# Attention scores as products of 128 key columns, added in PSUM to turned bias sums

## The chip, the cores and the metric

One core of one Trainium2 chip runs the whole kernel. The metric is device time in microseconds (us), the median of several runs. A profile is one further execution, recorded by the hardware profiler; its span is the recorded part of that execution.

## The reference

Four layers follow each other on an image `x` of 2 x 512 x 32 x 32 in f32. The change lies in the first, a deformable attention with 8 heads of 64 channels: 1024 queries per image (the pixels) and 64 keys per image and head (sampled points). Its core, shortened:

```python
pos = grid_q[:, :, None, :] - grid_kv[:, None, :, :]
bias = jnp.sign(pos) * jnp.log1p(jnp.abs(pos))
bias = jax.nn.relu(bias @ cpb_w1 + cpb_b1)      # 2 -> 128
bias = jax.nn.relu(bias @ cpb_w2 + cpb_b2)      # 128 -> 128
bias = (bias @ cpb_w3 + cpb_b3)                 # 128 -> 1, for each query and key
sim = jnp.einsum('bhid,bhjd->bhij', qh, kh) + bias
attn = jax.nn.softmax(sim, axis=-1)
out = jnp.einsum('bhij,bhjd->bhid', attn, vh)
```

So every pair of query and key goes through a small network of three layers, and its result is added to the product of query and key before the softmax. What follows is a projection and an MLP, a linear attention (layer 1), a full attention over 1024 positions (layer 2) and a rank-one attention with a gate (layer 3).

## The kernel before, in words

**Engines.** TensorE (PE) multiplies and writes PSUM; VectorE (DVE) and ScalarE (ACT) read PSUM and work elementwise; GpSimd (POOL) and SyncE (SP) issue DMAs here. On TensorE a weight load (PEld) puts the stationary operand (`lhsT`) in place, and the moving operand (`rhs`) streams past it. Each f32 matmul of the source stands in the trace as two instructions, a transpose as one.

**The loop.** The first layer is one loop over 512 keys, taken as 8 groups `g` of 64. A group is a pair of heads (`k`, 128 channels) of an image `b`, so every group holds 64 keys for each of two heads. Keys are taken two at a time as `p`; each half-step is written `(n, when)`, where `n` is the key and `when` 0 or 1. For each `p`:

- `first` (line 344, DVE, L349) makes the first layer of the bias network, two instructions per key;
- `second` (line 609) is called four times. Each call runs 8 matmuls (16 instructions, L616) with 32 stationary columns, four of which work side by side on quarters of the array, into `ph`, which has two buffers. ACT evicts `ph` with a ReLU into `r` (L625);
- `combine` (DVE, L631), `join`, `shift` and `fold` (DMAs that add on arrival, L634, L641, L646) fold the 128 hidden units together into tiles `xs`;
- `third` (line 664, PE, L669), every eighth key, multiplies by the last layer and adds four `xs` into the sums `psim0` and `psim1`, which hold 32 keys each: partition = key and head and half of the queries, column = query (512).

**Order.** Everything in the loop is pinned in program order. `at(n, when, fn)` puts a piece of work at a half-step, `run` carries it out there, so each engine sees the order of the calls. No planner moves it. After the loop `started.clear()` ends the pinning, and the last group's softmax runs with the work that follows.

**Around the change**, for a group `g`:

- `prepare` (line 679) samples and projects the keys. `keys` (line 733, ACT, L742) copies them, scaled, into `kblk`, and `values` (DVE, L754) copies the values. For `g > 0` the plan puts `keys` at key 64(g-1)+51. `kblk` has two sets (`g % 2`), each of four blocks of 128 columns: key half `kb`, query half `half`. It is zeroed once (line 149), so that each head meets its own channels only. `keys` fills it with 8 small copies.
- `scores` (line 648, PE, L654), at key 64g+10, multiplies `kblk` (stationary) by 512 queries of `q` (moving), 4 matmuls, and thereby starts `psim0` and `psim1`.
- `third` adds the bias sums to them (`start=False`) at keys 64g+14 to 64g+70.
- `attend` (line 793) is planned from key n = 64(g+1)+7. `evict` (ACT, L804) copies each `psim` to SBUF as `simt`, which lies in the same memory as `e`. `flip` (PE, L814) turns it by 8 transposes of 128 x 128 in two PSUM tiles `psm`, one for each key half, so that a query becomes a partition. `top` (DVE, L825) takes the maximum of each half, L827 the larger of the two, `sub` (DVE, L831) subtracts it into `e`; `exp` (ACT, L841), `total` (DVE, L845), `inverse` (L848) and `norm` (ACT, L852) complete the softmax. `back` (PE, L858) turns the result, and `keep_` (ACT, L867) writes it over the group's queries in `q`.
- While that goes on, `chain(1, 2, 82, 78)` and `chain(2, 4, 206, 114)` (lines 925 and 926) compute the sampling points of later groups: 36 pieces `tap` on DVE (L226, L229) over the keys 4 to 81 and 92 to 205, then short steps on ACT, DVE and PE.

After the loop, L1036 multiplies the probabilities kept in `q` by the projected values.

Of the kernel before, what the change touches and what calls it, by code (L numbers as in the profile page):

```python
# [10 lines left out]
F32 = mybir.dt.float32  # L11
AF = mybir.ActivationFunctionType
ALU = mybir.AluOpType
AX = mybir.AxisListType
PSUM = bass.MemoryType.PSUM

P = 128
B, C, H, W = 2, 512, 32, 32
HW = H * W
# [3 lines left out]
DH = 64  # L23
J = 64
# [47 lines left out]
def conv_seq(  # L72
# [20 lines left out]
    nc = tc.nc  # L93
# [6 lines left out]
    x = keep.tile([P, KC, NT], F32, name="x")  # L100
# [22 lines left out]
    ident = c("ident")  # L123
# [10 lines left out]
    with ExitStack() as ctx_l0:  # L134
        l0 = ctx_l0.enter_context(tc.tile_pool(name="l0", bufs=1))
        q = l0.tile([P, KC, NT], F32, name="q")


        kblk = l0.tile([P, 2, 2, 2, P], F32, name="kblk")
        vblk = l0.tile([P, 2, 2, J], F32, name="vblk")  # L140

        co = l0.tile([P, 2, 2, KC * B * J], F32, name="co")
# [43 lines left out]
        def pin(ins):  # L186
            return tc.keep_in_program_order(ins) if started else ins
# [406 lines left out]
        with tc.tile_pool(name="hid", bufs=3) as hid, tc.tile_pool(name="sm", bufs=1) as sm, tc.tile_pool(name="hps", bufs=2, space=PSUM) as hps, tc.tile_pool(  # L594
# [6 lines left out]
            def at(n, when, fn, *args):  # L601

                todo.setdefault((n, when), []).append((fn, args))
# [41 lines left out]
                for i in range(2):  # L645
                    pin(nc.gpsimd.dma_start(rs[p][i::2], r[i::2, i, :], accum_op=ALU.add))  # L646

            def scores(g):
                k, b = divmod(g, B)
                for kb in range(2):  # L650
                    ps = psims[g, kb] = sps.tile([P, 512], F32, name=f"psim{kb}")
                    for half in range(2):
                        pin(
                            nc.tensor.matmul(  # L654
                                ps,
                                lhsT=kblk[:, g % 2, kb, half, :],
                                rhs=q[:, k, b * HW + half * 512 : b * HW + (half + 1) * 512],
                                start=(half == 0),
                                stop=False,
                                skip_group_check=True,  # L660
                            )
                        )

            def third(g, u):
                kb, i = divmod(u, 4)
                p = (g * J + 8 * u) // 2
                for m in range(4):
                    pin(
                        nc.tensor.matmul(  # L669
                            psims[g, kb][m * 32 : (m + 1) * 32, :],  # L670
                            lhsT=cw3[:, 3 - i : 35 - i],
                            rhs=rs.pop(p + m),
                            start=False,
                            stop=(i == 3),
                            skip_group_check=True,
                        )
                    )

            def prepare(g):

                k, b = divmod(g, B)
                st = {}
# [49 lines left out]

                def keys():

                    for half in range(2):
                        for h in range(2):
                            hs = slice(h * DH, (h + 1) * DH)
                            for kb in range(2):
                                to = kblk[hs, g % 2, kb, half, :].rearrange("p (m s c i) -> p s m c i", m=4, s=4, c=2)
                                of = st["pk"][hs, 0, kb * 32 : (kb + 1) * 32]  # L740
                                pin(
                                    nc.scalar.activation(  # L742
                                        to[:, 2 * half + h],
                                        of.rearrange("p (i m c) -> p m c i", i=4, m=4),
                                        AF.Identity,
                                        scale=DH**-0.5,
                                    )
                                )

                def values():  # L750
                    for h in range(2):
# [41 lines left out]
            def attend(g, n, step):  # L793

                k, b = divmod(g, B)
                st = {}

                def evict(kb):
                    if kb == 0:

                        st["e"] = sm.tile([P, 16, J], F32, name="e")
                        st["simt"] = st["e"].rearrange("p s j -> p (s j)").rearrange("p (k n) -> p k n", k=2)
                    pin(
                        nc.scalar.activation(  # L804
                            st["simt"][:, kb, :], psims[g, kb], AF.Identity, bias=v("L0_conv_cpb_b3")
                        )
                    )

                def flip(kb):

                    pt = st["pt", kb] = mps.tile([P, 4, 4, 4, 8], F32, name="psm", tag="m")
                    for t in range(4):
                        pin(
                            nc.tensor.transpose(  # L814
                                pt[:, t].rearrange("p s m i -> p m s i"), st["simt"][:, kb, t * P : (t + 1) * P], ident
                            )
                        )

                def top(kb):
                    if kb == 0:  # L820
                        st["mx"] = sm.tile([P, 2, 16], F32, name="mx")
                        st["den"] = sm.tile([P, 16], F32, name="den")
                    mx = st["mx"]
                    pt = st["pt", kb].rearrange("p t s m i -> p (t s) (m i)")
                    pin(nc.vector.tensor_reduce(mx[:, kb, :], pt, AX.X, ALU.max))  # L825
                    if kb == 1:
                        pin(nc.vector.tensor_tensor(mx[:, 0, :], mx[:, 0, :], mx[:, 1, :], ALU.max))  # L827

                def sub(kb):
                    pin(  # L830
                        nc.vector.tensor_tensor(  # L831
                            st["e"][:, :, kb * 32 : (kb + 1) * 32],
                            st["pt", kb].rearrange("p t s m i -> p (t s) (m i)"),
                            st["mx"][:, 0, :].unsqueeze(2).to_broadcast([P, 16, 32]),
                            ALU.subtract,
                        )
                    )

                def exp(t):
                    es = st["e"][:, t * 4 : t * 4 + 4, :]  # L840
                    pin(nc.scalar.activation(es, es, AF.Exp))  # L841

                def total(i):
                    is_ = slice(8 * i, 8 * i + 8)
                    pin(nc.vector.tensor_reduce(st["den"][:, is_], st["e"][:, is_], AX.X, ALU.add))  # L845

                def inverse():
                    pin(nc.vector.reciprocal(st["den"], st["den"]))  # L848

                def norm(i):  # L850
                    e = st["e"][:, i]
                    pin(nc.scalar.activation(e, e, AF.Identity, scale=st["den"][:, i : i + 1]))  # L852

                def back(s):
                    pb = st["pb", s] = mps.tile([P, 512], F32, name="pb", tag="m")
                    for t in range(4):
                        pin(
                            nc.tensor.transpose(  # L858
                                pb[:, t * P : (t + 1) * P],
                                st["e"][:, 4 * t + 2 * s : 4 * t + 2 * s + 2].rearrange("p h j -> p (h j)"),  # L860
                                ident,
                            )
                        )

                def keep_(s):

                    pin(nc.scalar.copy(q[:, k, b * HW + s * 512 : b * HW + (s + 1) * 512], st["pb", s]))  # L867

                plan = [
                    (0, 0, evict, 0), (0, 1, evict, 1), (1, 1, flip, 0), (1, 1, flip, 1),  # L870
                    (2, 1, top, 0), (3, 1, top, 1), (4, 1, sub, 0), (6, 1, sub, 1),
                    (10, 1, exp, 0), (11, 1, exp, 1), (12, 1, exp, 2), (13, 1, exp, 3),
                    (14, 1, total, 0), (16, 1, total, 1), (17, 1, inverse),
                ]
                plan += [(19 + i // 2, i % 2, norm, i) for i in range(16)]
                plan += [
                    (29, 0, back, 0), (29, 0, back, 1), (29, 1, keep_, 0), (30, 1, keep_, 1),
                ]
                for dn, when, fn, *args in plan:
                    if step:  # L880
                        at(n + dn, when, fn, *args)
                    else:
                        fn(*args)
# [13 lines left out]
                    )  # L897
            for g in range(NG):
                prepare(g)
                at(J * g + 10, 0, scores, g)  # L900
                for u in range(8):
                    at(J * g + 8 * u + 14, 0, third, g, u)
                if g < NG - 1:
                    attend(g, J * (g + 1) + 7, True)
# [830 lines left out]
```

## Time and profile before

| What | us |
|---|---|
| median of 3 runs | 2767.3 |
| lowest and highest run | 2765.76, 2767.45 |
| the profiled execution | 2764.49 |
| its span | 2762.7 |

The granted TensorE clock in the profiled execution was 0.996. Groups that the change touches, with the sum of busy time and the mean length of one instruction, from the trace:

| Line | Engine | Work | Count | Busy us | Mean ns |
|---|---|---|---|---|---|
| L616 | PE | `second` | 16384 | 1790.7 | 593 |
| L654 | PE | `scores` | 64 | 29.6 | 605 |
| L814 | PE | `flip` | 64 | 8.9 | 280 |
| L669 | PE | `third` | 512 | 72.1 | 592 |
| L742 | ACT | `keys` | 64 | 8.7 | 184 |
| L825 | DVE | `top` | 16 | 11.0 | 688 |
| L827 | DVE | larger of two maxima | 8 | 1.4 | 175 |

A matmul's length in the trace includes its way through the array; matmuls overlap, so busy time is less than count times mean, and the distance between starts tells what one costs in a stream. A busy PE is not PE at its peak. Rows of the trace in order of time read: start, length, engine, line, operation, output and inputs, shapes, count, and in brackets the idle time before it with what ended it.

### The profile page before, as it was taken

How to read it: one execution, taken by the hardware profiler on the slowest of the kernel's cores; microseconds unless marked ns; L12 is line 12 of the kernel's file. 1: busy time of each engine (PE TensorE's matmuls, PEld its weight loads, DVE VectorE, ACT ScalarE, POOL GpSimd, SP SyncE). 2: the span in 40 equal slices, each digit the busy share in tenths (PEclk: the TensorE clock that was granted, in tenths of full speed). 3: DMA queues.
4: the chain of work that ended last, by engine and by line, in shares of the span. 5: the costliest groups of instructions: out<-in, count | busy, mean ns of one | idle time of the engine just before them, and what ended most of it. 6: DMA issues, size and time to landing. Idle time of an engine off the chain costs nothing.

```text
span 2762.7 us, 49727 instructions
## 1 busy us (share of the span) xinstructions
PE 2707.0 (98%) x19782; PEld 987.5 (36%) x19782; DVE 2266.7 (82%) x2473; ACT 1544.3 (56%) x1950; POOL 663.6 (24%) x776
## 2 busy tenths in 40 slices
PE   8999999999999999999999999999999999999996
PEld 4233323233332323333333333333344444455543
DVE  6999999999999999999999999999654545523555
ACT  6676677667667776766776676676321111001244
POOL 0333333333333333333333333333100000000000
PEclk9999999999999999999999999999999999999998
DMA  3777777777777777777787778777400000100001
GB/s 121 160 163 155 161 154 160 158 160 158 154 164 149 162 163 158 161 161 156 167 185 172 152 165 193 154 170 159 102 30 23 16 23 23 70 7 0 0 1 61
DMA packets 145479, 335.14 MB, mean 121 GB/s; under 512 B 22592, under 2 KB 32064, under 8 KB 144480
## 3 DMA queue, kind: packets, MB, share of 16 engines
q0 software_dynamic: 77824, 201.38, 41.1%
q1 hardware_dynamic: 66992, 130.08, 13.2%
q8 instruction: 156, 2.56, 0.4%
q14 instruction: 75, 0.61, 0.1%
q10 hardware_dynamic: 432, 0.51, 0.1%
HBM read 58.99 MB, written 4.46 MB: 23 GB/s over the span
## 4 chain that ended last, share of the span: by engine, by line
PE 93%; ACT 3%; DVE 2%; issue 1%; DMA 1%; ACTq 0%; DVEq 0%; POOL 0%; SPq 0%; POOLq 0%
PE ph L616 61%; PE A L1101 4%; PE D L1101 4%; PE C L1101 4%; PE psim L669 2%; PE pr L1348 2%; PE B L1101 2%; PE po L1036 2%; PE pg L1244 1%; PE psim L654 1%; PE pz L1450 1%; PE pa L1339 1%; PE pu L1278 1%; ACT r L625 1%; PE pscore L1421 1%
## 5 line engine op out<-in xcount | busy, mean ns | idle before, releaser
L616 PE MATMUL ph<-h,w2a 128*32 128x512 f32 x16384 | 1790.7, 593 | 7.0 <-ACT r L625 6.9
L625 ACT ACTIVATE r<-ph,sb 128x1024 f32<-128x1024 f32 x1024 | 1141.4, 1115 | 562.3 <-PE ph L616 541.1
L349 DVE CUSTOM_DVE_ANT_1 h<-tab 128x1024 f32<-128x1024 f32 x1024 | 1205.9, 1220 | 8.6 <-PE ph L616 4.7
L616 PEld LDWEIGHTS ph<-h,w2a 128*32 128x32 f32 x16384 | 533.5, 109 | 1217.5 <-issue 833.1
L631 DVE SCALAR_TENSOR_TENSOR r<-r,rel,r 128x1024 f32<-128x1024 f32 x512 | 656.0, 1281 | 28.0 <-ACT r L625 27.3
L646 POOL DMA_DIRECT2D xs<-r x512 | 476.9, 1144 | 196.0 <-PE ph L616 95.7
L634 POOL DMA_DIRECT2D r<-r x256 | 222.2, 868 | 1107.2 <-DVE r L631 931.1
L172 ACT ACTIVATE tab<-tab,vec 128x256 f32<-128x256 f32 x252 | 137.1, 544 | 0.0
L1289 POOL MEMSET M<- 128x512 f32 x2 | 1.0, 520 | 439.6 <-DVE x L1165 439.6
L1141 ACT COPY u<-A 128x512 f32<-128x512 f32 x16 | 9.4, 585 | 146.9 <-PE A L1101 146.9
L1120 ACT ACTIVATE h<-h,vec 128x512 f32<-128x512 f32 x32 | 23.1, 721 | 113.6 <-DVE h L1123 113.6
L669 PE MATMUL psim<-xs,cw 128*32 128x512 f32 x512 | 72.1, 592 | 2.1 <-DMA xs<-r 2.1
L1123 DVE TENSOR_TENSOR h<-C,u 128x512 f32<-128x512 f32 x32 | 22.1, 691 | 48.8 <-PE C L1101 48.5
L1101 PE MATMUL A<-xn,w 128*128 128x512 f32 x128 | 60.2, 593 | 0.8 <-DVE x L1043 0.8
L1101 PE MATMUL C<-hT,w 128*128 128x512 f32 x128 | 60.3, 592 | 0.0
L1101 PE MATMUL A<-h,w 128*128 128x512 f32 x128 | 60.1, 592 | 0.0
L1036 PE MATMUL po<-q,vwo 128*128 128x512 f32 x128 | 56.4, 594 | 0.0
L1348 PE MATMUL pr<-x,A 128*128 128x512 f32 x128 | 55.1, 592 | 0.0
L229 DVE SCALAR_TENSOR_TENSOR acc<-q,vec,acc 128x128 f32<-128x128 f32 (+3 forms) x88 | 46.2, 525 | 0.8
L1161 DVE TENSOR_TENSOR x<-D,x 128x512 f32<-128x512 f32 x32 | 22.1, 691 | 26.0 <-PE D L1101 26.0
L852 ACT ACTIVATE e<-e,den 128x64 f32<-128x64 f32 x128 | 41.7, 336 | 2.7 <-DVE den L848 2.7
L1161 DVE TENSOR_TENSOR x<-C,x 128x512 f32<-128x512 f32 x32 | 22.1, 690 | 24.8 <-PE C L1101 24.8
(288 smaller groups left out, 1770.3 us busy)
## 6 DMA issues: line engine op xcount, KB each, us to landing
r<-r POOLq DMA_DIRECT2D x256, 512.0 KB, 4.7
xs<-r SPq DMA_DIRECT2D x512, 128.0 KB, 2.4
xs<-r POOLq DMA_DIRECT2D x512, 128.0 KB, 4.8
tab<-fd SPq DMA_DIRECT2D x63, 512.0 KB, 6.0
lw<-in_l_w_dram SPq DMA_DIRECT2D x5, 1024.0 KB, 10.2
x<-in_x_dram SPq DMA_DIRECT2D x4, 1024.0 KB, 8.5
w<-in_mlp_w_dram SPq DMA_DIRECT2D x8, 512.0 KB, 4.2
w<-in_mlp_w_dram SPq DMA_DIRECT2D x16, 256.0 KB, 3.2
```

The lines of the kernel that those rows point to most:

```text
L172: return nc.scalar.activation(tf, tf if src is None else src[:, :, :, ax, :], AF.Identity, bias=0.0 if ax == 0 else v("L0_conv_cpb_b1"), s ...
L229: pin(nc.vector.scalar_tensor_tensor(dst, src, wt_, dst, ALU.mult, ALU.add))
L349: nc.vector._custom_dve(TENSOR_ADD_SAT, out=h1[:, h], in0=tab[:, j, h, 0, :].unsqueeze(1).to_broadcast([P, 32, 32]), in1=tab[:, j, h, 1, : ...
L616: nc.tensor.matmul(ph[t * 32 : (t + 1) * 32, i, :], lhsT=w2a[:, o], rhs=h1s[2 * p + i][:, h, half * 512 : (half + 1) * 512], start=True, s ...
L625: pin(nc.scalar.activation(r, ph, AF.Relu, bias=sb3[:, o, 1:2]))
L631: pin(nc.vector.scalar_tensor_tensor(r0, r1, rel[:, i : i + 1], r0, ALU.mult, ALU.add))
L634: pin(nc.gpsimd.dma_start(rs[p, 0], rs.pop((p, 2)), accum_op=ALU.add))
L646: pin(nc.gpsimd.dma_start(rs[p][i::2], r[i::2, i, :], accum_op=ALU.add))
L669: nc.tensor.matmul(psims[g, kb][m * 32 : (m + 1) * 32, :], lhsT=cw3[:, 3 - i : 35 - i], rhs=rs.pop(p + m), start=False, stop=(i == 3), ski ...
L1036: nc.tensor.matmul(po, lhsT=vwo[:, k * B + t // 2, o * P : (o + 1) * P], rhs=q[:, k, ts_], start=(k == 0), stop=(k == KC - 1),)
L1101: nc.tensor.matmul(banks[bank], lhsT=a[an][k], rhs=b_[bn_][k], start=(i < 4 and k == 0), stop=(k == n - 1), skip_group_check=True,)
L1348: nc.tensor.matmul(pr, lhsT=A[b][:, k, o * P : (o + 1) * P], rhs=x[:, k, ns], start=(k == 0), stop=(k == KC - 1),)
```

## The change

Queries become the stationary operand. For each of the 8 blocks of 128 queries, one product of 128 queries by 128 key columns (64 for each head) is added in PSUM to what the transposes have just put there. `scores` goes, `third` starts the sums itself, `kblk` shrinks to one block of 128 columns per set, filled by two copies in place of eight, and the tiles of `flip`, `top` and `sub` are split by queries (`i`) in place of key halves, so that all 64 keys of a query lie in one tile and the merge of the two maxima goes. The plan's half-steps stay: both `flip` calls at (1, 1), `top` at (2, 1) and (3, 1), `sub` at (4, 1) and (6, 1).

```diff
-        kblk = l0.tile([P, 2, 2, 2, P], F32, name="kblk")
+        kblk = l0.tile([P, 2, 2, J], F32, name="kblk")
...
-            def scores(g):
...
             def third(g, u):
...
+                if i == 0:
+                    psims[g, kb] = sps.tile([P, 512], F32, name=f"psim{kb}")
...
-                            start=False,
+                            start=(i == 0),
...
                 def keys():
-                    for half in range(2):
-                        for h in range(2):
-                            hs = slice(h * DH, (h + 1) * DH)
-                            for kb in range(2):
...
+                    for h in range(2):
+                        hs = slice(h * DH, (h + 1) * DH)
+                        pin(
+                            nc.scalar.activation(
+                                kblk[hs, g % 2, h, :].rearrange("p (k x i) -> p k x i", k=2, i=4),
+                                st["pk"][hs, 0, :].rearrange("p (k i x) -> p k x i", k=2, i=4),
...
+                def flip(i):
+                    pt = st["pt", i] = mps.tile([P, 2, 4, J], F32, name="psm", tag="m")
+                    for t in range(2):
+                        at_ = (2 * i + t) * P
+                        for kb in range(2):
+                            pin(
+                                nc.tensor.matmul(
+                                    pt[:, t, :, kb * 32 : (kb + 1) * 32].rearrange("p s (m i) -> p m s i", m=4),
+                                    lhsT=st["simt"][:, kb, at_ : at_ + P],
+                                    rhs=ident,
+                                    start=(t == 0 and kb == 0),
+                                    is_transpose=True,
+                                    stop=False,
...
+                        for half in range(2):
+                            to = b * HW + half * 512 + at_
+                            pin(
+                                nc.tensor.matmul(
+                                    pt[:, t, 2 * half : 2 * half + 2].rearrange("p h j -> p (h j)"),
+                                    lhsT=q[:, k, to : to + P],
+                                    rhs=kblk[:, g % 2].rearrange("p h j -> p (h j)"),
+                                    start=False,
+                                    stop=True,
...
-                    if kb == 1:
-                        pin(nc.vector.tensor_tensor(mx[:, 0, :], mx[:, 0, :], mx[:, 1, :], ALU.max))
...
-                at(J * g + 10, 0, scores, g)
```

More of the change, by code (lines that the diff above doesn't have):

```diff
@@ L646, in fold @@
                     pin(nc.gpsimd.dma_start(rs[p][i::2], r[i::2, i, :], accum_op=ALU.add))
-            def scores(g):
-                k, b = divmod(g, B)
-                for kb in range(2):
-                    ps = psims[g, kb] = sps.tile([P, 512], F32, name=f"psim{kb}")
-                    for half in range(2):
[L653 to L662, printed above, removed]
             def third(g, u):
@@ L733, in keys @@
                 def keys():
-                    for half in range(2):
-                        for h in range(2):
-                            hs = slice(h * DH, (h + 1) * DH)
[L738 to L748, printed above, removed]
+                    for h in range(2):
[4 more added lines that the diff above has]
+                                st["pk"][hs, 0, :].rearrange("p (k i x) -> p k x i", k=2, i=4),
+                                AF.Identity,
+                                scale=DH**-0.5,
+                            )
+                        )
                 def values():
@@ L807, in evict @@
                     )
[L809 to L815, printed above, removed]
-                            )
[L817 to L821, printed above, removed]
-                        st["den"] = sm.tile([P, 16], F32, name="den")
-                    mx = st["mx"]
-                    pt = st["pt", kb].rearrange("p t s m i -> p (t s) (m i)")
-                    pin(nc.vector.tensor_reduce(mx[:, kb, :], pt, AX.X, ALU.max))
-                    if kb == 1:
-                        pin(nc.vector.tensor_tensor(mx[:, 0, :], mx[:, 0, :], mx[:, 1, :], ALU.max))
@@ L829, in sub @@
-                def sub(kb):
+                def flip(i):
[11 more added lines that the diff above has]
+                                    stop=False,
+                                    skip_group_check=True,
+                                )
+                            )
+                        for half in range(2):
[7 more added lines that the diff above has]
+                                    stop=True,
+                                    skip_group_check=True,
+                                )
+                            )
@@ L830, in sub, with top @@
+                def top(i):
+                    if i == 0:
+                        st["mx"] = sm.tile([P, 2, 8], F32, name="mx")
+                        st["den"] = sm.tile([P, 16], F32, name="den")
+                    pt = st["pt", i].rearrange("p t s j -> p (t s) j")
+                    pin(nc.vector.tensor_reduce(st["mx"][:, i, :], pt, AX.X, ALU.max))
+                def sub(i):
                     pin(
                         nc.vector.tensor_tensor(
-                            st["e"][:, :, kb * 32 : (kb + 1) * 32],
@@ L833, in sub @@
-                            st["pt", kb].rearrange("p t s m i -> p (t s) (m i)"),
-                            st["mx"][:, 0, :].unsqueeze(2).to_broadcast([P, 16, 32]),
+                            st["e"][:, 8 * i : 8 * i + 8],
+                            st["pt", i].rearrange("p t s j -> p (t s) j"),
+                            st["mx"][:, i, :].unsqueeze(2).to_broadcast([P, 8, J]),
                             ALU.subtract,
```

## The prediction

> **What bounds the kernel now.** I read the page's first part, then busy time by stretches of the span, then the order of time on TensorE around one group's softmax, then what VectorE waits for. On the page TensorE (PE) is busy nearly always and VectorE (DVE) most of the time:
>
> ```profile
> PE 2707.0 (98%) x19782; PEld 987.5 (36%) x19782; DVE 2266.7 (82%) x2473; ACT 1544.3 (56%) x1950; POOL 663.6 (24%) x776
> ```
>
> That average mixes stages. By stretches of 200 us (columns: PE, PEld, DVE, ACT, POOL busy, each with its count; granted clock; DMA share; GB/s):
>
> ```profile
> 100.00:300.00 200.00, 199.55 (x1854) 63.93 (x1850) 199.47 (x195) 139.00 (x157) 71.31 (x83) 1.00 0.76 163
> 500.00:700.00 200.00, 199.47 (x1809) 65.48 (x1802) 199.54 (x188) 144.28 (x172) 68.54 (x81) 1.00 0.73 156
> 900.00:1100.00 200.00, 199.55 (x1838) 61.53 (x1834) 192.45 (x173) 139.54 (x162) 68.81 (x80) 1.00 0.75 160
> 1100.00:1300.00 200.00, 199.55 (x1838) 61.53 (x1834) 192.43 (x173) 141.97 (x175) 69.37 (x82) 1.00 0.74 159
> ```
>
> The reader is to see two stages in the loop over 512 keys (47 to about 1955 us). Up to about 850 us, while `Chain.tap` (lines 215 to 229) also runs on DVE, DVE has no idle time: time saved on PE there comes back as PE waiting for DVE. After it DVE has 7.6 us in 200 to spare, and PE alone sets the pace: scores start at 1050.59 and again at 1287.07 in the chain, 236.5 us apart, in every later group too.
>
> One group on PE, in order of time (start, length, line, count):
>
> ```profile
> 309.03 8.77 PE L616 MATMUL ph<-h,w2a 128*32 128x512 f32 x80
> 317.73 1.09 PE L814 MATMUL psm<-cst,e 128*128 128x128 f32 x8
> 318.75 5.36 PE L616 MATMUL ph<-h,w2a 128*32 128x512 f32 x48
> 324.04 3.70 PE L654 MATMUL psim<-q,kblk 128*128 128x512 f32 x8
> 327.67 0.64 PE L616 MATMUL ph<-h,w2a 128*32 128x512 f32 x4
> ```
>
> Without interruption L616 takes 0.429 us for each four instructions (in the chain 27.47 us for 256). So 80 of them stream for 8.58 us, to 317.61, and the next start at 318.75: **the flip costs PE 1.14 us**, 8 transposes at 0.109 (0.87) and 0.27 for going into and out of the full array. 48 more stream to 323.90, and the next begin at 327.67: **the scores cost 3.77 us** (4 matmuls in the source, 8 instructions, since each f32 product appears as two: 8 x 0.429 = 3.43, and 0.34 around them).
>
> **The change part by part.**
>
> *Scores removed:* 3.77 us of PE for each of 8 groups, 30.2 in all.
>
> *Products added to the flip:* 2 x 2 x 2 matmuls of 128 stationary by 128 moving columns, 16 instructions a group. Their nearest rows have this shape: L542 in the prologue, followed there by a transpose, and L1407 late in the kernel (8 at 2599.40, the next matmul at 2600.29: 0.111 each).
>
> ```profile
> 30.09 2.05 PE L542 MATMUL pfb<-cst,acc 128*128 128x128 f32 x16 [0.78 <-DVE acc L279]
> 31.98 0.27 PE L322 MATMUL pft<-cst,acc 128*128 128x128 f32 x1
> ```
>
> Between its later instructions L542 steps by 0.111 us, and the transpose behind it starts 0.112 after the last: neither the weight load (0.19 us, twice as many as before) nor the change from product to transpose costs extra. In the other direction, L858 to L1036, the product starts 0.109 after the transpose (1982.64 to 1982.75). So 16 x 0.111 = **1.8 us a group**, with nothing more for entering the full array, which the flip did anyway. Bounds: 16 x 0.107 = 1.7 below (the bare stream, a quarter of 0.429); above, 16 x 0.19 = 3.1 (L498, full-array products with strided operands, step by 0.19). I take L542, which has the shape and contiguous operands. No row shows a product added on top of a transpose; that is priced among the rivals.
>
> [...]
>
> *Keys:* 8 ACT instructions become 2.
>
> ```profile
> 967.61 1.12 ACT L742 ACTIVATE kblk<-pk 64x32 f32<-64x32 f32 x8
> 968.75 2.12 ACT L625 ACTIVATE r<-ph,sb 128x1024 f32<-128x1024 f32 x2
> 968.76 0.46 DVE L754 COPY vblk<-pk 64x64 f32<-64x64 f32 x2 [1.94 <-ACT kblk L742]
> 969.92 0.16 PEld L616 LDWEIGHTS ph<-h,w2a 128*32 128x32 f32 x8 [1.36 <-ACT r L625]
> ```
>
> The eight hold up the eviction of `ph` (L625), and PE gets its next buffer at 969.92 where its stream ended at 969.29: 0.6 us lost in each group. Two 64x64 instructions at the 0.245 of L852 (128x64, 16 in 3.93) are 0.5 in place of 1.12, so the 0.6 goes. Bounds: 0 to 0.65.
>
> *Softmax on DVE:* the two maxima and subtractions keep 512 elements each (0.69 and 0.68); the merge L827 (0.18) goes. `flip(0)` now waits for both evictions: the second ends at 316.12, PE comes to the flip at 317.6, so 1.5 us cover it; without that cover the 0.68 of an eviction would be the price. Queued behind it are L616's next products, for which ACT's eviction waits. The first `top` starts at 322.41, so a flip 1.8 us longer (to 320.5) is still in time. `third` starts its own sums: same instructions. The memset of `kblk` halves (0.95 us on POOL at 0.7, with no waiter). No DMA is added or moved.
>
> *Sum, PE stage (key 206 on):* 4 scores at -3.77 = -15.1; 4 flips and the last group's, +1.8 each = +9.0; 4 keys at -0.6 = -2.4. Together **-8.5 us**. The last flip runs among L1036's products, which keep PE full: its 64 instructions that need nothing of that group last to 1990.6, the turned probabilities are there at 1985.8, so a chain 2 us later is hidden.
>
> *Sum, DVE stage:* only what shortens DVE's own row counts. Its waits from 47 to 860 us:
>
> ```profile
> DVE r L631 <- ACT r L625: 3.6, 5, 1.7
> DVE vblk L754 <- ACT kblk L742: 1.5, 3, 0.5
> DVE vblk L754 <- issue: 1.2, 1, 1.2
> ```
>
> Of the first, 1.68, 0.80 and 0.39 come right behind the scores of groups 0 to 2, when PE gives ACT nothing for 3.98 us: 2.9 goes. The longer flips (2.94) stay under the 3.77 that caused it. Keys: 1.5 and 0.6 of the 1.2. The merge: 3 x 0.18 = 0.5. Together -5.5; I take **-5**, as some of it precedes waits of the chain at 837 to 850 that stay. Bounds: 0, and PE's whole saving there, 4 x 3.77 - 3 x 1.8 + 3 x 0.6 = 11.5.
>
> **Sum:** -13.5 us. The profiled execution took 2764.5 (span 2762.7 and 1.8 around it), so 2751.0; the median of the runs lies 2.8 above it: **2754 us** on that scale.
>
> **The rivals.**
>
> *The whole PE saving comes through:* -8.5 - 11.5 = -20, **2747**. For it: PE is at 99.8% in the early stretches too, and the chain is almost all L616. Against: DVE at 99.7% there.
>
> *Nothing comes through before 850 us:* -8.5, **2759**. For it: the stalls at 837 to 850 are a chain over ACT's tables that may swallow all that is ahead of them.
>
> *The new products don't run into one another (the slower side):* a load that can't go ahead gives 0.19 + 0.107 = 0.30 a pass, 4.75 us a group: the PE stage comes to -15.1 + 5 x 4.75 - 2.4 = +6.3, the DVE stage keeps about -1.5, **2772**. [...] If each pass besides waits until the sum below it is written (0.19 + 0.275, L542's own duration), 7.4 us a group: +19.7 and about +4, **2791**. It is slower than before from 0.24 us a pass on. For it: no row adds products to transposes in one bank. Against: L1407 adds four products on one sum at 0.111.
>
> *Each change between transposes and products drains the array:* 0.275 - 0.109 = 0.166 for 7 changes a group, 1.2 us; the PE stage falls to -2.7, all to -7.7, **2760**. Against: L542 to L322.
>
> *PE's saving returns as a wait elsewhere in the second stage:* about **2766**. DVE's spare 7.6 us in 200 speaks against it, and DMA at 0.75 of its time too.
>
> **How the numbers follow.** Chances: forecast 0.45, all of PE 0.12, late stage alone 0.16, drains 0.07, returned 0.10, not run together 0.10. Measurements tell this kernel from no change at about 0.2%, 5.5 us. Faster by more (under 2761.8): the first four less a little that falls short, 0.77; same 0.12; slower 0.11. The range leaves out the extreme lower edge and the serial cases: 2747 to 2768.
>
> **What would show it.** Starts of the flips' instructions 0.11 us apart, a flip of 2.9 us between two L616; no scores; 0.5 us of keys with no PE gap behind; 234 us from group to group after 1050 us, not 236.5; DVE at over 99% still before 850 us, and the time at key 206 some 5 us earlier. It would be wrong if the products step by 0.24 us or more, or if the later groups do not get shorter.

## The result and the profile after

| What | before | after |
|---|---|---|
| median of 4 runs each, us | 2766.62 | 2747.66 |
| lowest and highest run, us | 2765.76, 2767.45 | 2746.91, 2750.04 |
| the profiled execution, us | 2764.49 | 2746.91 |
| its span, us | 2762.7 | 2745.1 |

The ratio of after to before is 0.9933, with a 95% interval of 0.9922 to 0.9945: the kernel became faster by 0.7%, some 18.5 us (15 to 21.6). The forecast of 2754 has the right sign and lies 6.3 us too high; 2747.66 is 0.66 above the lower end of its range.

Where the 17.6 us between the two profiled executions lie comes from the times at which TensorE starts a key's first `second`, read from both traces:

| Stretch | before | after | difference | forecast |
|---|---|---|---|---|
| start to key 0 | 47.0 | 46.4 | -0.6 | 0 |
| key 0 to key 208 | 782.7 | 773.5 | **-9.2** | **-5** |
| key 208 to the last `second` | 1124.4 | 1113.8 | -10.6 | -10.3 |
| from there to the first product of the MLP | 65.5 | 68.4 | +2.9 | +1.8 |
| rest | 743.2 | 743.0 | -0.2 | 0 |

(The forecast's -8.5 for the PE stage is -15.1 + 7.2 - 2.4 = -10.3 for the loop and +1.8 for the last flip behind it.) A second profile of each kernel gives 784.2 and 774.0, and 1124.4 and 1113.8, for the two long stretches, 65.3 and 68.8 for the one behind the loop.

The page and the stretches of 200 us for after (columns as for before: PE, PEld, DVE, ACT, POOL busy, granted clock, DMA share, GB/s):

```profile
PE 2693.7 (98%) x19846; PEld 1003.0 (37%) x19846; DVE 2262.8 (82%) x2465; ACT 1540.5 (56%) x1902; POOL 662.2 (24%) x776
```

```profile
100.00:300.00 200.00, 200.00 (x1847) 72.36 (x1842) 199.94 (x195) 137.99 (x150) 69.62 (x81) 1.00 0.76 163
500.00:700.00 200.00, 199.45 (x1836) 69.22 (x1832) 199.97 (x188) 142.88 (x170) 67.94 (x79) 1.00 0.75 159
...
1100.00:1300.00 200.00, 200.00 (x1870) 62.83 (x1866) 194.64 (x174) 143.16 (x170) 69.91 (x82) 1.00 0.76 163
```

PE's busy time fell by 13.3 us, DVE's by 3.9. In the early stretches (the first two rows) both engines are now busy to the last 0.3%; in before DVE had 0.46 to 0.53 idle in the same windows. After key 208 DVE has 5 us in 200 to spare.

The flip of one group on PE in after, in order of time:

```profile
308.50 5.33 PE L615 MATMUL ph<-h,w2a 128*32 128x512 f32 x48
313.77 0.44 PE L797 MATMUL psm<-cst,e 128*128 128x128 f32 x2
314.04 0.61 PE L810 MATMUL psm<-kblk,q 128*128 128x128 f32 x4
...
316.04 0.61 PE L810 MATMUL psm<-kblk,q 128*128 128x128 f32 x4
316.58 14.80 PE L615 MATMUL ph<-h,w2a 128*32 128x512 f32 x136
```

Two transposes, then four instructions of products (two for each of two f32 products), four times over. Eight transposes and 16 of these stand between 313.65 (308.50 and 12 times 0.429) and 316.58, so the flip costs PE 2.93 us; 2.94 was forecast. No row has a bracket: nothing waited. From group to group the later flips start 233.84 us apart:

```profile
1033.77 0.44 PE L797 MATMUL psm<-cst,e 128*128 128x128 f32 x2
...
1267.61 0.44 PE L797 MATMUL psm<-cst,e 128*128 128x128 f32 x2
```

The two copies of the keys, in the same places of the loop as before's eight:

```profile
957.82 0.43 ACT L723 ACTIVATE kblk<-pk 64x64 f32<-64x64 f32 x2
...
958.28 1.11 ACT L624 ACTIVATE r<-ph,sb 128x1024 f32<-128x1024 f32 x1
958.29 0.46 DVE L735 COPY vblk<-pk 64x64 f32<-64x64 f32 x2 [1.25 <-ACT kblk L723]
```

They take 0.43 where the eight took 1.12, and PE streams L615 through this place (954.78 to 962.26) without a gap. What DVE waits for from 47 to 860 us:

```profile
DVE acc L278 <- ACT acc L275: 2.3, 2, 2.1
DVE acc L257 <- ACT acc L250: 1.4, 1, 1.4
...
DVE r L630 <- ACT r L624: 0.4, 1, 0.4
```

The 3.6 us that DVE waited for ACT's `r` are 0.4 now, and the waits for ACT's `kblk` are gone. What is left belongs to the chains of sampling points, which the change does not touch.

### The profile page after: what moved, and what is told of

The parts are those of the page before. It is cut to its first block, busy times and chain, and to the rows that moved or that the text cites. A ratio compares the mean times of both kernels' runs of the same rounds, so it can differ in the third digit from the quotient of the medians.

```text
span 2745.1 us, 49805 instructions
## 1 busy us (share of the span) xinstructions
PE 2693.7 (98%) x19846; PEld 1003.0 (37%) x19846; DVE 2262.8 (82%) x2465; ACT 1540.5 (56%) x1902; POOL 662.2 (24%) x776
## 4 chain that ended last, share of the span: by engine, by line
PE 93%; DVE 4%; ACT 2%; issue 1%; DMA 0%; ACTq 0%; DVEq 0%; POOL 0%; POOLq 0%
PE ph L615 61%; PE A L1098 4%; PE D L1098 4%; PE C L1098 4%; PE po L1033 2%; PE psim L654 2%; PE pr L1345 2%; PE B L1098 2%; DVE h L348 1%; PE pg L1241 1%; PE pa L1336 1%; PE pz L1447 1%; PE pu L1275 1%; PE pscore L1418 1%; DVE r L630 1%
## 5 line engine op out<-in xcount | busy, mean ns | idle before, releaser
L615 PE MATMUL ph<-h,w2a 128*32 128x512 f32 x16384 | 1792.0, 593 | 3.4 <-ACT r L624 3.3
L615 PEld LDWEIGHTS ph<-h,w2a 128*32 128x32 f32 x16384 | 545.1, 109 | 1203.2 <-issue 805.2
L630 DVE SCALAR_TENSOR_TENSOR r<-r,rel,r 128x1024 f32<-128x1024 f32 x512 | 654.5, 1278 | 12.2 <-ACT r L624 11.6
```

What stands on the lines that cost most here:

```text
L615: nc.tensor.matmul(ph[t * 32 : (t + 1) * 32, i, :], lhsT=w2a[:, o], rhs=h1s[2 * p + i][:, h, half * 512 : (half + 1) * 512], start=True, s ...
L630: pin(nc.vector.scalar_tensor_tensor(r0, r1, rel[:, i : i + 1], r0, ALU.mult, ALU.add))
```

## The experiments

What had to be explained is the early stage: 9.2 us where the forecast had 5. The times of the stretch from key 72 to key 208 (three flips and, in before, three scores, two copies of keys) are compared below; it took 515.5 us in before and 509.7 in after, in both profiles of each. Theory A is the forecast's: DVE sets the pace there, and PE's instructions count only where DVE waits for them. Theory B is its rival: PE sets the pace there too. Where an expectation of the first four runs names a third case, it is that run's own; theory C of the last two was formed after the others. Differences to after are against its 2747.66.

### Eight copies of the keys again

```diff
-                                kblk[hs, g % 2, h, :].rearrange("p (k x i) -> p k x i", k=2, i=4),
...
+                        for kb in range(2):
+                            for xs_ in (slice(0, 4), slice(4, 8)):
+                                pin(
+                                    nc.scalar.activation(
+                                        to[:, kb, xs_], of[:, kb, xs_], AF.Identity, scale=DH**-0.5
```

> The changed kernel, with the keys copied into kblk by 8 ACT instructions again (64x16 each) in place of 2. Theory A (in the second stage, from key 208 on, TensorE alone sets the pace and the eight copies hold up the eviction of ph; before key 208 VectorE sets it, and waits for those copies): every later group loses 0.66 us on TensorE, 4 x 0.66 = 2.6, and VectorE's waits at the values come back before key 208, 1.5 to 2.1. Together 4 to 5 us over the changed kernel's 2747.7: 2752. Rival B (the copies were never on the path, all the gain is TensorE's products): 2748, and group to group 233.8 us as in the changed kernel, where A says 234.5.

Measured: 2749.89 us (2749.70 to 2752.53), ratio to before 0.9943 (0.9926 to 0.9959), 2.2 above after. The copies in its trace, in order of time:

```profile
962.12 0.77 ACT L727 ACTIVATE kblk<-pk 64x16 f32<-64x16 f32 x8
```

Eight copies of 16 columns take 0.77, not the 1.12 of before's eight with 32 columns. The later groups are 234.16 us long, 0.32 more than in after, close to the 0.34 by which ACT's copies are longer; the early stretch takes 510.2, +0.5. So ACT's time at this place does come back as PE's time, about one for one. The run restores only half of what before lost here, so the forecast's 0.6 a group is confirmed in kind only. Its size is no direct measurement but a remainder: the 0.66 that is left of the 2.64 between a group's 236.48 and 233.84 once the scores and the products (-3.77 + 1.79) are taken out.

### The scores put back, dead

Four products of 128 x 512 at the old place, with the identity in the keys' stead; `third` starts its sums anew, so they change nothing.

```diff
+            def scores(g):
...
+                                lhsT=ident,
...
-                if i == 0:
-                    psims[g, kb] = sps.tile([P, 512], F32, name=f"psim{kb}")
...
+                at(J * g + 10, 0, scores, g)
```

> The changed kernel with the old four products of 512 columns a group put back at their old place as dead work: they write the sums that the first bias product then starts anew (stationary operand: the identity). Key copies and flip stay as changed. Theory A (VectorE sets the pace before key 208): from key 208 on 4 x 3.77 = +15.1 us; before it not 4 x 3.77 = 15.1 but only what VectorE waits behind these products, 5 to 7. Total 2768 (2766 to 2770). Rival B (TensorE sets the pace all along): +30, 2778.

Measured: 2775.70 us (2774.75 to 2778.18), ratio 1.0038 (1.0023 to 1.0053), 28.0 above after, for eight times 3.77 = 30.2. The later groups are 237.6 us, +3.8 as forecast. From key 72 to 208 it takes 519.6: +9.9 of the 11.3 that three scores cost PE. Theory A allowed only DVE's waits behind them. It falls here; B's figure is the near one.

### The products left out

The products of queries and keys are not computed; the bias sums alone are turned and go into the softmax.

```diff
-                                    stop=False,
...
-                                    lhsT=q[:, k, to : to + P],
-                                    rhs=kblk[:, g % 2].rearrange("p h j -> p (h j)"),
...
+                                    stop=(t == 1 and kb == 1),
```

> The changed kernel without the 16 product instructions of each flip: the product of queries and keys is left out of the scores, everything else stays. Prices the added part. Theory A: from key 208 on 4 flips and the last one shorter by 16 x 0.111 = 1.8 us, -8.9; before key 208, where VectorE sets the pace, 0 to -1.5. Total 2738 (2737 to 2739). Rival B (TensorE sets the pace all along): three more times -1.8, 2733. Rival C (the products do not run into one another, 0.2 us or more each): -16 and more after key 208, under 2732.

Measured: 2738.10 us (2735.66 to 2740.06), ratio 0.9900 (0.9885 to 0.9915), 9.6 below after. The later groups take 232.1 us, so 16 instructions of products cost 1.79 (1.8 was forecast). But from key 72 to 208 the time falls by only 1.3 (to 508.4) of the 5.4 that PE saves there. Now B falls: taking PE time away does little, though adding it counted almost in full.

### Each maximum taken three times

```diff
-                    pin(nc.vector.tensor_reduce(st["mx"][:, i, :], pt, AX.X, ALU.max))
+                    for _ in range(3):
+                        pin(nc.vector.tensor_reduce(st["mx"][:, i, :], pt, AX.X, ALU.max))
```

> The changed kernel with each maximum of top taken three times in place of once: 4 more VectorE instructions of 0.69 us a group, 2.8 us, as dead work; nothing on TensorE or ScalarE. Theory A (VectorE sets the pace before key 208, and has some 4 us to spare in every 200 after it): groups 0 to 2 take their softmax before key 208, so 3 x 2.8 = +8.3 there, 0 after it, about 1 in the tail behind the loop: 2756 to 2757. Rival B (TensorE sets the pace all along): no change, 2748.

Four more instructions of 0.69 us a group, 2.76 us of DVE. Measured: 2759.83 us (2756.98 to 2763.79), ratio 0.9978 (0.9969 to 0.9988), 12.2 above after. From key 72 to 208: 517.0, +7.3 of 8.3. So adding to DVE counts there as well. In the later groups, where DVE has some 6 us to spare, it costs 1.0 a group (234.8); A had nothing there.

### The dead products elsewhere, twice

If both engines hold when something is added, the place might decide: PE could have a reserve away from the old place of the scores. The dead products went into a tile of their own, at another key.

```diff
+                ps = mps.tile([P, 512], F32, name="dead", tag="m")
...
+                at(J * g + 36, 1, scores, g)
```

> As dead_scores (the changed kernel with four dead products of 512 columns a group), but at key 64g+36, far from the flip at 64g+8, and into a free PSUM tile. Theory A, now with a reserve (VectorE sets the pace before key 208; it has about 4.2 us of work in hand, so that a block on TensorE of up to that length leaves it no idle time, and of a longer one it idles the rest): 3.77 us alone is covered, so the stretch from key 72 to key 208 takes 510 to 512 us as in the changed kernel (509.7), where dead_scores, whose block lay beside the flip, took 519.6. From key 208 on 5 x 3.77 = +18.9. Total 2768 to 2770. Rival B (TensorE's whole work sets the pace there too, wherever it lies): the stretch takes 509.7 + 2 x 3.77 = 517, total 2776 to 2778.

Measured: 2787.16 us (2786.77 to 2787.50), ratio 1.0075 (1.0059 to 1.0090). The edit brought a wait of its own: in seven groups the dead products stood until `keep_` had copied the first half of the group before out of its PSUM tile, with PE idle for 1.7 us each time. With it they cost 5.55 us in a later group (239.40), so the run doesn't test a block of 3.77.

Five keys later (`at(J * g + 41, 1, scores, g)`, else the same) that wait is gone:

> As dead_scores_apart, but at key 64g+41, where no other work holds the PSUM tiles (at 64g+36 the products stood 2.16 us waiting for ScalarE to empty a tile, so that the block was 5.9 us and not 3.77, and the run could not tell the theories apart). Theory A with a reserve: a block of 3.77 us alone leaves VectorE next to no idle time, so key 72 to key 208 takes 510 to 512 us, and the groups after key 264 take 3.77 more each, 237.6. Total 2767 to 2770. Rival B (TensorE's work shows wherever it lies): key 72 to 208 takes 517, total 2776 to 2778.

Measured: 2774.97 us (2774.28 to 2778.82), ratio 1.0032 (1.0020 to 1.0044). From key 72 to 208, 516.0: +6.3 of the 7.5 of the two that fall in it; 237.6 in the later groups. There is no reserve at this place either.

### Lighter VectorE, with and without the products

What fits all of this is theory C: PE and DVE have rows of nearly the same length in this stretch (a row is an engine's work there end to end), and between the points where both wait for ACT the longer row counts. Then a cut on one alone gives little, and cuts on both give everything. First DVE alone: the two copies behind the keys go to ACT, the maxima are not taken, and zeros are subtracted in their place: 5.5 us less for DVE (six maxima of 0.69, and 1.4 of copies).

```diff
-                    pin(nc.vector.tensor_copy(st["kv"], st["pkv"]))
+                    pin(nc.scalar.copy(st["kv"], st["pkv"]))
...
-                            nc.vector.tensor_copy(
+                            nc.scalar.copy(
...
-                        st["mx"] = sm.tile([P, 2, 8], F32, name="mx")
+                        st["mx"] = zero
...
-                    pin(nc.vector.tensor_reduce(st["mx"][:, i, :], pt, AX.X, ALU.max))
```

> As values_on_scalar, and without the maxima: top is left out and zeros are subtracted in place of the largest score of a query. VectorE's row is shorter by 3 x 1.38 + 2 x 0.68 = 5.5 us between key 72 and key 208, TensorE's row as in the changed kernel. Theory C (TensorE and VectorE have rows of nearly the same length there, and in each stretch between two places where both wait for ScalarE the longer one counts; in the changed kernel the two are within some 1.5 us): TensorE's row is what is left, key 72 to 208 takes 508.2 to 509.1 (changed kernel 509.7). Theory A (VectorE alone sets the pace there): 504 to 505. After key 208 no change.

Measured: 2748.02 us (2747.58 to 2748.26), ratio 0.9936 (0.9914 to 0.9959), no different from after. From key 72 to 208: 508.4, -1.3 of the 5.5 us. Theory A, by which all of it had to come through, falls a second time.

Then the same with the products left out too:

> As light_vector, and without the 16 product instructions of each flip (the product of queries and keys is left out too). Both rows are shorter by some 5.4 us between key 72 and key 208. Theory C: now the stretch shortens by more than the two edits alone gave together (1.3 for no_products, 0.6 to 1.5 for light_vector): 504 to 506. Theory A: as light_vector, 504 to 505. If it stays above 507, something else than these two rows sets the pace there. After key 208 the groups take 232.1 us, as in no_products.

Measured: 2732.79 us in both runs, ratio 0.9881 (0.9852 to 0.9909). From key 72 to 208: 504.3. Apart, the two cuts gave 1.3 and 1.3; **together they give 5.4**. Neither A nor B has room for that; a pair of rows does.

The same stretch in five traces, busy time by engine (columns as above); the length of the stretch less DVE's busy time is what DVE sat idle. Before:

```profile
314.20:829.70 515.50, 511.56 (x4644) 164.18 (x4639) 511.21 (x491) 363.42 (x440) 176.77 (x206) 1.00 0.74 158
```

After:

```profile
310.20:819.90 509.70, 506.65 (x4667) 168.09 (x4663) 508.71 (x486) 362.56 (x428) 175.65 (x205) 1.00 0.75 159
```

Without the products:

```profile
312.30:820.70 508.40, 505.66 (x4620) 167.96 (x4616) 507.85 (x486) 362.53 (x428) 175.51 (x204) 1.00 0.74 159
```

With the lighter DVE:

```profile
311.40:819.90 508.50, 505.46 (x4671) 163.24 (x4667) 504.60 (x475) 363.28 (x434) 175.97 (x206) 1.00 0.75 159
```

With both:

```profile
309.90:814.20 504.30, 501.22 (x4620) 160.46 (x4616) 503.37 (x474) 363.42 (x434) 175.75 (x204) 1.00 0.75 160
```

DVE's idle time is 4.3, 1.0, 0.5, 3.9 and 0.9 us. Where it is about 4 us, PE's row is the longer one; where it is 1 us or less, DVE's row has been met. Put in numbers: take 508.4 as PE's row in after (from the light DVE, where DVE has time to spare) and 508.4 as DVE's (from the run without products, where DVE has none). Each edit adds its price to one row (in before three scores at 3.77, less three times 1.79 of products, two copies of keys at 0.66, three merges at 0.18), and the longer row is set beside the measured time:

| Kernel | PE's row | DVE's row | longer | measured |
|---|---|---|---|---|
| before | +11.3 - 5.4 + 1.3 = 515.6 | +0.5 = 508.9 | 515.6 | 515.5 |
| dead scores | +11.3 = 519.7 | 508.4 | 519.7 | 519.6 |
| dead scores five keys later | +7.5 = 515.9 | 508.4 | 515.9 | 516.0 |
| maxima three times | 508.4 | +8.3 = 516.7 | 516.7 | 517.0 |
| after | 508.4 | 508.4 | 508.4 | 509.7 |
| eight copies | +0.7 = 509.1 | 508.4 | 509.1 | 510.2 |
| light DVE and no products | -5.4 = 503.0 | -5.5 = 502.9 | 503.0 | 504.3 |

Where the rows differ by 6.7 us or more, the longer one gives the time to 0.3. Where they are within 1 us, 1.1 to 1.3 more is lost, since now one and now the other is late between two meeting points. The two starting values were fitted to two of the runs; the seven rows of the table were not. (The dead products that waited fit as well: two at the 5.55 of a later group give 519.5, and 519.6 was measured.) Such a row is a length worked out from edits and not DVE's busy time: in before DVE was busy for 511.2 us of the stretch, 2.3 more than its row, mostly because it had one more `r` (1.3 us) and one more step of the chain (0.4 us) done by the time PE came to key 208. Only this stretch was tested so. The one from key 0 to 72 was not: it became 3.4 us shorter, with DVE's idle time down from 4.1 to 1.2, which fits theory C but doesn't test it.

### Two versions that follow

The two copies alone moved from DVE to ACT (`values` half a key later), with the maxima kept:

```diff
-                    pin(nc.vector.tensor_copy(st["kv"], st["pkv"]))
+                    pin(nc.scalar.copy(st["kv"], st["pkv"]))
...
-                        (16, 1, sample), (18, 0, got), (19, 1, project), (21, 0, keys), (21, 1, values),
+                        (16, 1, sample), (18, 0, got), (19, 1, project), (21, 0, keys), (22, 0, values),
```

> The changed kernel with the copies of the sampled keys and of the values moved from VectorE to ScalarE, the values one half-step later than the key copies. Theory A: before key 208 VectorE's row shortens by 0.22 + 0.46 us a group for the groups 1 to 3, some 2 us, and the wait before the values goes, 0.5; after key 208 nothing, as VectorE has time to spare there and 0.46 us on ScalarE is less than the 0.66 that cost TensorE 0.6. Total 2745 to 2746. Rival B (TensorE sets the pace all along): 2747.7 or above.

Measured: 2746.26 us (2744.43 to 2748.93), ratio 0.9928 (0.9915 to 0.9940), not to be told from after. From key 72 to 208 it takes 509.0, -0.7 of the 1.4 expected there, as two rows of one length would have it.

The same, and two of the output products of the first image (16 instructions, 6.9 us) moved ahead of the last bias products, where PE waits for a DMA:

```diff
+            early = hps.tile([P, 2, 512], F32, name="ph")
...
+                            rhs=q[:, k, 0:512],
...
+                if t == 0 and o < 2:
+                    continue
```

> As values_on_scalar, and behind the last key two of the output products (16 instructions of 0.43 us, 6.9 us) stand ahead of the last bias products, whose data a DMA still brings: TensorE waited 2.0 us for it there, and in the changed kernel's profile the granted clock was 0.5 for the 3.4 us after that wait. If the wait is on the path, 2 us go, and 1.7 more where the clock fell: 2742 (2741 to 2744). Rival (the last group's softmax behind those bias products is the path, and gets later): 2746 or above.

Measured: 2744.27 us (2742.36 to 2744.55), ratio 0.9918 (0.9904 to 0.9931): the fastest version of these. Behind the loop it takes 65.1 us, 3.3 less than after. Of that, 1.4 lies between after and the version with the copies alone (67.0), in whose profile the first 16 output products took 7.03 us, without the fall of the granted clock that made them 8.62 in after; 1.9 is the edit, near the 2.0 expected. PE still waits for 0.84 us there. The median lies just above the expected 2741 to 2744 and 3.4 below after's, but the intervals of the ratios overlap.

Both kernels once more, for the stage times above:

> The kernel before once more, to see whether the fall of the granted clock behind the loop (0.5 for 3.4 us in the changed kernel and in four experiments, not in the one profile of before) belongs to the change. If it belongs to the wait of 2.7 us for the last DMA, which both kernels have, before shows it too in some executions; if it belongs to the change, not.

> The changed kernel once more on the chip of the run beside it. Expected as before, 2746 to 2750. The groups after key 264 take 233.8 us each again. If the clock's fall behind the loop is not tied to the change, it can be missing this time, and the stretch from the last key's products to the MLP is then 66.7 us in place of 68.4.

Measured: 2766.13 us for before (one run) and 2748.66 (2747.27 to 2749.47) for after, ratio 0.9937 (0.9925 to 0.9950). Both long stretches repeat to 1.5 us, the one from key 72 to 208 to 0.1. Behind the loop the first 16 output products again took longer in after (8.23 us) than in before (7.03), behind waits for the last DMA of 2.12 and 2.13 us. (The 2.7 us of the expectation is what the last bias product waited for DMA in the run with the dead scores.)

## Why the prediction was right in its sign and short in its size

**Scores removed: right.** 3.77 us a group, confirmed by the dead ones (+3.8 in the later groups).

**Products added: right.** 1.79 us a group for 1.8; the flip took 2.93 for 2.94. Products run straight onto transposes in the same PSUM tile, 0.11 us apart: the rivals of serial products (2772 to 2791) and of drains at each change of kind (2760) are out. The loads of L810 take 0.19 us each, and its products still start 0.11 us apart, so the loads are not added to the products' time here.

**Keys: right.** 0.43 us for the forecast 0.5, no gap on PE, and 0.66 a group, as the remainder, for 0.6. (The prediction has the memset of `kblk` halved; the tile has a quarter of the columns, and 0.95 us became 0.31.)

**PE stage: right by group, short by 1.1 behind the loop.** 233.84 a group for 234. The last flip made the stretch behind the loop some 1.5 longer (67.0 in the kernel with the copies on ACT, where the clock did not drop, against 65.5), near the 1.8 forecast. The rest of the +2.9 is the granted clock, which no step of the forecast had. The first output products behind the loop in after, on PE in order of time:

```profile
1937.19 1.02 PE L654 MATMUL psim<-xs,cw 128*32 128x512 f32 x2 [2.03 <-DMA xs<-r]
...
1938.52 8.62 PE L1033 MATMUL po<-q,vwo 128*128 128x512 f32 x16
```

The same in the kernel with the copies on ACT:

```profile
1937.19 7.03 PE L1033 MATMUL po<-q,vwo 128*128 128x512 f32 x16
```

The same 16 instructions take 8.62 us in the one and 7.03 in the other. In after PE had waited 2.03 us for the last DMA, and from 1938.3 to 1941.7 the records give a clock of 0.5; the window row there shows it:

```profile
1935.00:1945.00 10.00, 7.97 (x17) 3.37 (x17) 2.03 (x2) 0.51 (x1) 3.31 (x6) 0.83 0.65 144
```

The wait alone doesn't decide it: in both profiles of before PE waits as long at this place (2.12 and 2.13 us), and the 16 products take 7.03 us; in the first the clock stays at 1.00 from 1955 to 1975. Here is the first of them:

```profile
1957.60 1.02 PE L669 MATMUL psim<-xs,cw 128*32 128x512 f32 x2 [2.12 <-DMA xs<-r]
...
1959.04 7.03 PE L1036 MATMUL po<-q,vwo 128*128 128x512 f32 x16
```

In the second profile of after they take 8.23 us behind a wait of 2.12; in the kernel with the copies on ACT they take 7.03 behind a wait of the same 2.12. What decides whether the clock falls was not shown, and as that kernel has the change too and kept its clock, no run shows that the change has a part in it.

**DVE stage: wrong, and this is the step that failed.** The prediction said "only what shortens DVE's own row counts" and priced it at 5 us from the list of DVE's waits behind scores and keys; 9.2 was measured. It read DVE's 99.7% as the mark of the engine that sets the pace. But PE stood at 99.8% in the same rows, and both can't be read as the bound by that share. In before it was PE's row that was longer, by 6.7 us from key 72 to 208 (515.6 against 508.9), while DVE sat idle for 4.3 us of that stretch in waits spread over several lines. The change took 7.2 us off PE's row. DVE's row stopped it 5.8 us down, with 1.0 us idle left to it.

The bound that the prediction gave for the other side, PE's whole saving of 11.5, was not reached either. That the rival "the whole PE saving comes through" names 2747 and 2747.66 was measured is a sum of other parts: early 2.3 less than its 11.5, the last stretch 1.1 worse, and 1.1 better in the loop's later part, the prologue and the rest, on top of a median that lies 0.75 over the profile where 2.8 was allowed. That 2747.66 still lies inside the forecast's range is in part luck too: in the profiled execution the fall of the clock added some 1.4 us, twice its distance from the range's lower end.

The claim that DVE would stay at over 99% before 850 us held, and could not tell the theories apart: it holds under A and under C. The claim that key 206 would come some 5 us earlier could, and failed.

## What to carry to other kernels

Where two engines are both busy to 99% in a stage, neither share says which one sets the pace: saving on one comes through until its row meets the other's, so compare the saving with all of the other's idle time in that stage (4.3 us in 515 here, of which 1.0 is left), not only with the waits next to the edit. To find out, cut each engine alone and then both: 1.3 and 1.3 us apart and 5.4 together is what two rows of one length look like here, and adding to either is then paid almost in full. A saving that goes past the meeting point is lost unless the other row is cut as well, which is where the next change has to begin.

## What the runs showed of the hardware that was not expected

A wait of some 2 us on TensorE was followed by the same 16 output products at two speeds: 8.62 and 8.23 us in the two profiles of after (waits of 2.03 and 2.12), 7.03 in both of before and in the kernel with the copies on ACT (2.12, 2.13 and 2.12). In the first of these the granted clock was 0.5 for 3.4 us (1938.3 to 1941.7), and 1.6 us were lost on the 16 products. The length of the wait does not tell the two cases apart, since 2.12 us stands in both; what does was not shown.

Where VectorE had some 6 us to spare in a group, 2.76 us more on it still cost 1.0 us of the group's time: spare time on an average is not spare time at the place where it is needed.
